# Seven products for the gated blocks of the last stage, with sums of sign matrices kept on chip

## The chip, the cores and the metric

The kernel runs on one core of one Trainium2 chip. The metric is the device time of one execution in microseconds (us). TensorE (PE) multiplies, VectorE (DVE), ScalarE (ACT) and GpSimd (POOL) do elementwise work, SyncE (SP) issues most DMAs. All data are float32.

## The reference

For x of 4 x 512 tokens and 1024 features, with 16 heads of 64:

```python
xn = layernorm(x)
s = attention(xn @ Wq, xn @ Wk, xn @ Wv) @ Wo        # rotary on q and k, causal
routing = softmax(xn @ gate_w.T)                     # 8 experts
in_scale, out_scale = routing @ in_channel_scale, routing @ out_channel_scale
g = silu(((xn * in_scale) @ sign(weight).T) * out_scale + bias)
out = x + s * g
```

The change is in the gated product `(xn * in_scale) @ sign(weight).T`, and in how its results and those of `@ Wo` are put together.

## The kernel before

**Stages.** For each of the four sequences the kernel normalizes and transposes x (and spills it as `xn_d`), projects queries, keys and values, and computes scores, probabilities and values, which it spills as `at_d`. Projections and attention are interleaved on TensorE: `interleave` deals the matmuls of the projections evenly between the "pieces" of the attention of the group before (scores, transposes, values). The projections and the product with Wo are already done by Strassen's scheme in the form with seven products: quarters of the left operand give sums S1 to S4, quarters of the right one T1 to T4, and the products 1 to 7 are combined through partial sums u2 = product 1 + product 6 and u3 = u2 + product 7.

**The last stage** works on eight pairs of row tiles (128 tokens each; a pair is `pairs[q] = (b, t)`, its tiles `t` and `t + 2` of sequence `b`). Pairs 0 and 1 have their gated product computed among the last pieces of attention. From then on, pair after pair:

- `project_out(q)`: seven products of the attention output with Wo. Each is four float32 matmuls of 512 columns, and each such matmul shows as two passes in the trace. `finish` adds the partial sums, multiplies by the gate Z and adds the residual x (`XR`), and a DMA writes the rows out.
- Between those products, `in_scales(q + 1)` scales the inputs of the next pair (`XP`) by the routing, `split` writes each as a high and a low float32r part (`hi` by ScalarE, `lo` by VectorE as input minus high part), and `out_scales` puts the output scales into Z.
- `gated(q + 1)`: for each of the four blocks (row tile i, column half k) `ffn` sums 8 chunks x 2 parts = 16 float32r matmuls of 512 columns with the stored signs `sg[0..7]` in one PSUM bank. VectorE then multiplies the bank by Z, POOL adds the bias, ScalarE takes the sigmoid, POOL multiplies.

**What sets the order.** TensorE's order is that of the program text (`manual_schedule`). The other engines are ordered by a scheduler, except for instructions under `keep_in_program_order`. Each engine works in order, so an instruction that waits holds up all behind it; SP's DMA queue is such a line too. Buffers come from pools with a fixed number of places: four PSUM banks for `bank` (the ring), four for Wo's products (`ps_wo`), one place for XP, two for the attention output (`ap0` and `app`, pairs taking turns), two each for `hi`, `lo`, `xr`, `c` and `g`.

Of the kernel before, what the change touches and what calls it, by code (L numbers as in the profile page):

```python
# [9 lines left out]
F32 = mybir.dt.float32  # L10
F32R = mybir.dt.float32r
AF = mybir.ActivationFunctionType
ALU = mybir.AluOpType
# [38 lines left out]
def attn_gated_ffn_kernel(  # L52
# [705 lines left out]
    def split(q, i):  # L758

        HI[q, i] = hl.tile([P, NC, P], F32R, tag="hi", name=f"hi_{q}_{i}")  # L760
        LO[q, i] = hl.tile([P, NC, P], F32R, tag="lo", name=f"lo_{q}_{i}")
        for c in range(0, NC, 4):
            xs, hi, lo = (v[:, c : c + 4, :] for v in (XP[q][:, i], HI[q, i], LO[q, i]))
            nc.scalar.copy(hi, xs)
            nc.vector.tensor_tensor(lo, xs, hi.bitcast(F32), op=ALU.subtract)


    z_place = {}
# [108 lines left out]
    for k, (b, g) in enumerate(groups):  # L877
        pieces = []
        if k > 0:
            pieces, late = attention_pieces(k - 1, late)  # L880
        extra = []
        if g == 0:
            routing = [lambda n=n: router(b, n) for n in range(3)]
            if k == 0:
                nothing = lambda: None
                pieces = [
                    routing[0],
                    lambda: (load_scales(in_scale), load_scales(out_scale)),
                    routing[1],
                    nothing,  # L890
                    routing[2],
                    lambda: split_scales(isc),
                    nothing,
                    nothing,
                    nothing,
                ]
            else:

                if b < B - 1:
                    pieces.insert(7, routing[0])  # L900
                pieces.insert(10, routing[1])
                pieces.insert(13, routing[2])
        elif g == 1 and b + 1 < B:

            pieces.insert(12, lambda: [load_x(b + 1, t) for t in range(2)])
            if b == 0:
                pieces.insert(6, lambda: split_scales(osc))
        elif g > 1 and b + 1 < B:
            t0 = 2 * (g - 2)
            for t in range(t0, t0 + 2):  # L910
                layernorm(b + 1, t)
            extra = [
                lambda t=t, h=h: transpose_x(b + 1, t, h) for t in range(t0, t0 + 2) for h in range(2)
            ]
            if g == 2:
                extra.append(lambda: [load_x(b + 1, t) for t in (2, 3)])

        step = max(1, (len(pieces) + len(extra)) // (len(extra) + 1))
        for n, e in enumerate(extra):
            pieces.insert(min(len(pieces), (n + 1) * step + n), e)  # L920
        if len(pieces) > 18:

            pieces.append(lambda: None)
        if k in (5, 9, 12, 13):
            n = {5: 0, 9: 2, 12: 4, 13: 6}[k]
            pieces.insert(8, lambda: make_sign(n + 1))
            pieces.insert(4, lambda: make_sign(n))
            pieces.insert(0, lambda: (load_sign(n), load_sign(n + 1)))
        if b == B - 1:

            if g < 2:
                load_xn(g)
            if g in (1, 2):
                pieces.insert(3, lambda: in_scales(g - 1, score_banks))
            if g == 3:
                z_place[0] = [xip.tile([P, E], F32, tag="x", name=f"z0_{i}") for i in range(2)]
                pieces.insert(3, lambda: out_scales(0, score_banks))
        if k == 11:

            pieces.append(lambda: router(b + 1, 0))  # L940
        interleave(pieces, fill, 3 * 7 * 4 if k else 3 * 7 * 4 - 8)
        if g == NGRP - 1:
            for _ in fill:
                pass
            if b + 1 < B:
                for n in (3, 1, 2, 4):
                    form_x(b + 1, n)
                fill = projections(b + 1)
# [45 lines left out]
    def ffn(q, i, k):  # L994

        cols = slice(k * HALF, (k + 1) * HALF)
        acc = bank(f"ff_{q}_{i}_{k}")
        for c in range(NC):
            for part in (HI, LO):
                nc.tensor.matmul(  # L1000
                    acc,
                    lhsT=part[q, i][:, c, :],
                    rhs=sg[4 * k + c // 2][:, (c % 2) * HALF : (c % 2 + 1) * HALF],
                    start=(c == 0 and part is HI),
                    stop=(c == NC - 1 and part is LO),
                )
            if c % 2 and c < NC - 1:
                yield
        z = Z[q, i][:, cols]
        nc.vector.tensor_tensor(z, acc, z, op=ALU.mult)  # L1010
        nc.gpsimd.tensor_tensor(z, z, bias_sb[:, cols], op=ALU.add)
        if q > 1:
            silu(q, i, k)
        yield

    def silu(q, i, k):
        z = Z[q, i][:, k * HALF : (k + 1) * HALF]
# [8 lines left out]

    def load_at(q):
        b, t = pairs[q]
        place = app if q % 2 else ap0
        AP_[q] = place.tile([P, 2, NC, P], F32, tag="ap", name=f"ap_{q}")  # L1030
        for i in range(2):
            nc.sync.dma_start(out=AP_[q][:, i].rearrange("p c q -> p (c q)"), in_=at_d[b, t + 2 * i])
# [57 lines left out]
    xsp = pool(side="right", name="xs", bufs=1)  # L1090
    work = pool(side="right", name="work", bufs=2)
    sp = pool(side="right", name="strassen", bufs=1)
    ps_wo = pool(side="right", name="ps_wo", bufs=4, space=PSUM)

    def form_a(q, n):
# [6 lines left out]
            3: lambda: (a11, a21, ALU.subtract),  # L1102
            4: lambda: (a12, SA[q, 2], ALU.subtract),
        }[n]()
        nc.vector.tensor_tensor(s, x0, x1, op=op)

    def project_out(q):

        b, t = pairs[q]
        rows = [slice((b * TPB + t + 2 * i) * P, (b * TPB + t + 2 * i + 1) * P) for i in range(2)]  # L1110
        for i in range(2):
            XR[i] = work.tile([P, E], F32, tag="xr", name=f"xr_{q}_{i}")
            nc.sync.dma_start(out=XR[i], in_=x[rows[i], :])
        a11, a12, a21, a22 = (AP_[q][:, i, 4 * f : 4 * f + 4, :] for i in range(2) for f in range(2))

        def product(n, lhs, rhs):
            ps = ps_wo.tile([P, HALF], F32, tag="wo", name=f"wo_{q}_{n}")
            for k in range(4):
                nc.tensor.matmul(ps, lhsT=lhs[:, k, :], rhs=rhs[:, k, :], start=(k == 0), stop=(k == 3))  # L1119
            return ps  # L1120

        def part(n):
            return sp.tile([P, HALF], F32, tag=f"part{n}", name=f"part_{q}_{n}")

        def finish(i, k, ps, u):
            cols = slice(k * HALF, (k + 1) * HALF)
            c = work.tile([P, HALF], F32, tag="c", name=f"c_{q}_{i}_{k}")
            z = Z[q, i][:, cols]
            nc.vector.tensor_tensor(c, ps, u, op=ALU.add)
            nc.vector.tensor_tensor(z, c, z, op=ALU.mult)  # L1130
            nc.gpsimd.tensor_tensor(z, z, XR[i][:, cols], op=ALU.add)

        def ahead_of(i, k, u):

            cols = slice(k * HALF, (k + 1) * HALF)
            c = work.tile([P, HALF], F32, tag="g", name=f"uz_{i}_{k}")
            nc.gpsimd.tensor_tensor(c, u, Z[q, i][:, cols], op=ALU.mult)
            nc.gpsimd.tensor_tensor(c, c, XR[i][:, cols], op=ALU.add)
            return c

        def finish_last(i, cols, ps, c, queue):
# [3 lines left out]
            queue.dma_start(out=out[rows[i], cols], in_=z)  # L1145

        yield
        ps = product(1, a11, b11)
        p1 = part(1)
        nc.scalar.copy(p1, ps)  # L1150
        ps = product(2, a12, b21)
        finish(0, 0, ps, p1)
        yield
        ps = product(6, SA[q, 2], t2)
        u2 = part(2)
        nc.vector.tensor_tensor(u2, ps, p1, op=ALU.add)
        ps = product(7, SA[q, 3], t3)
        u3 = part(3)
        nc.vector.tensor_tensor(u3, ps, u2, op=ALU.add)
        yield  # L1160
        last = q == len(pairs) - 1
        if last:
            nc.sync.dma_start(out=out[rows[0], :HALF], in_=Z[q, 0][:, :HALF])
            c10 = ahead_of(1, 0, u3)
        ps = product(5, SA[q, 1], t1)
        p5 = part(5)
        nc.scalar.copy(p5, ps)
        finish(1, 1, ps, u3)
        nc.gpsimd.tensor_tensor(u2, u2, p5, op=ALU.add)
        yield  # L1170
        ps = product(4, a22, t4)
        if not last:
            finish(1, 0, ps, u3)
            nc.gpsimd.dma_start(out=out[rows[1], :], in_=Z[q, 1])
            ps = product(3, SA[q, 4], b22)
            finish(0, 1, ps, u2)
            nc.gpsimd.dma_start(out=out[rows[0], :], in_=Z[q, 0])
            return
        c01 = ahead_of(0, 1, u2)
# [22 lines left out]
            for k in range(2):  # L1202
                silu(q, i, k)
    for q in range(len(pairs)):
        for n in range(1, 5):
            form_a(q, n)
        if q + 1 < len(pairs):
            load_at(q + 1)
        ahead = []
        if 1 <= q < len(pairs) - 1:  # L1210
            ahead = [
                lambda: None,
                lambda: (in_scales(q + 1), split(q + 1, 0), split(q + 1, 1)),
                lambda: out_scales(q + 1),
            ]
        for _ in project_out(q):
            if ahead:
                ahead.pop(0)()
        if 1 <= q < len(pairs) - 1:
            if q + 2 < len(pairs):  # L1220
                load_xn(q + 2)
            for _ in gated(q + 1):
                pass


def _rotary_tables():
# [55 lines left out]
```

## Time and profile before

| | |
|---|---|
| median of 3 runs | 1176.7 us (1176.45 to 1176.75) |
| the profiled execution | 1177.4 us, span 1175.7 us |
| busy: TensorE, weight loads | 1166.3 us (99%), 859.9 us (73%) |
| busy: VectorE, ScalarE, POOL | 754.8 us (64%), 488.0 us (42%), 555.2 us (47%) |
| granted TensorE clock | 1.0 |
| last stage, from the first product with Wo | 883.85 us to the end |
| one pair there | 39.8 us: gated 14.5, products with Wo 24.4, scales 0.9 |

Busy time is summed by engine over the span. TensorE's instructions overlap, so a busy TensorE is not one at its peak; what an instruction of it costs is read from how far a stage advances per instruction. Idle time of an engine that is not the bottleneck costs nothing by itself.

### The profile page before, as it was taken

The page shows a single profiled execution, that of the slowest core. Times are in us where ns is not written, and L with a number is a line of the kernel's source. Part 1 is how long each engine was busy: PE and PEld are TensorE (multiplying, and loading weights), DVE is VectorE, ACT ScalarE, POOL GpSimd, SP SyncE. Part 2 cuts the span into 40 slices and gives each one's busy share as a digit, 9 for nine tenths or more (in the row PEclk, how much of TensorE's full clock was granted, in tenths as well). Part 3 has the DMA queues.
Part 4 walks back from the last instruction along what each step waited for, and adds up shares of the span by engine and source line. Part 5 has one row for each costly group of instructions (what it writes and reads, how often), then busy time and mean ns, then how long its engine had stood idle before and what let it go on. Part 6 is the DMA issues. An engine that isn't in the chain of part 4 may idle for free.

```text
span 1175.7 us, 16090 instructions
## 1 busy us (share of the span) xinstructions
PE 1166.3 (99%) x5864; PEld 859.9 (73%) x5864; DVE 754.8 (64%) x1380; ACT 488.0 (42%) x1115; POOL 555.2 (47%) x597
## 2 busy tenths in 40 slices
PE   9999999999999999999999999999999999999998
PEld 8878787877878787877878787787774556655664
DVE  7876677568768667776877776665856543453343
ACT  2552673363366435436653453564532221222120
POOL 0661654264255435524643552374446445543544
PEclk9999999999999999999999999999999999999999
DMA  8413423222242232224227212211404513432320
GB/s 309 134 37 105 146 94 94 91 84 81 81 162 81 67 132 83 81 81 145 60 84 243 83 63 81 81 50 55 179 15 165 191 56 108 148 114 70 108 72 36
DMA packets 60015, 121.92 MB, mean 104 GB/s; under 512 B 5024, under 2 KB 40608, under 8 KB 53920
## 3 DMA queue, kind: packets, MB, share of 16 engines
q1 hardware_dynamic: 55072, 112.11, 28.8%
q0 software_dynamic: 4576, 8.39, 2.1%
q8 instruction: 46, 0.75, 0.2%
q10 hardware_dynamic: 288, 0.39, 0.1%
q14 instruction: 33, 0.27, 0.1%
HBM read 95.45 MB, written 25.43 MB: 103 GB/s over the span
## 4 chain that ended last, share of the span: by engine, by line
PE 96%; DVE 2%; ACT 1%; issue 1%; POOL 0%; DVEq 0%; POOLq 0%; ACTq 0%
PE pj L342 31%; PE wo L1119 16%; PE pj L429 16%; PE ff L1000 10%; PE sc L517 6%; PE pv L599 6%; PE ptp L583 6%; PE xtp L210 1%; PE idle L791 1%; PE lg L622 1%; ACT p L535 0%; DVE S L296 0%; PE os L774 0%; PE is L746 0%; DVE w L296 0%
## 5 line engine op out<-in xcount | busy, mean ns | idle before, releaser
L545 POOL TENSOR_SCALAR p<-p,rs 128x128 f32<-128x128 f32 (+3 forms) x256 | 170.3, 678 | 263.5 <-DVE rs L543 263.4
L535 ACT ACTIVATE p<-sc,nmx 128x128 f32<-128x128 f32 (+3 forms) x256 | 132.7, 524 | 155.1 <-DVE nmx L532 145.2
L342 PE MATMUL pj<-X,w 128*128 128x256 f32 x576 | 138.3, 381 | 0.2 <-ACT X L216 0.2
L326 POOL TENSOR_TENSOR sw<-sw,sin_sb 128x512 f32<-128x512 f32 x64 | 87.6, 1369 | 94.8 <-ACT sw L324 81.6
L342 PE MATMUL pj<-T,S 128*128 128x256 f32 x512 | 123.7, 382 | 0.0
L342 PEld LDWEIGHTS pj<-X,w 128*128 128x128 f32 x576 | 105.1, 190 | 14.4 <-issue 1.8
L342 PE MATMUL pj<-T,w 128*128 128x256 f32 x448 | 107.3, 381 | 0.0
L589 ACT COPY pT<-ptp 128x512 f32<-128x512 f32 x96 | 56.1, 586 | 119.4 <-PE ptp L583 118.9
L532 DVE TENSOR_REDUCE nmx<-sc 128x2 f32<-128x512 f32 (+3 forms) x128 | 103.7, 820 | 2.8
L1000 PE MATMUL ff<-sg,hi 128*128 128x512 f32 x256 | 103.3, 404 | 0.0
L342 PEld LDWEIGHTS pj<-T,S 128*128 128x128 f32 x512 | 93.2, 190 | 13.6 <-issue 1.4
L1000 PE MATMUL ff<-sg,lo 128*128 128x512 f32 x256 | 99.8, 390 | 0.0
L429 PE MATMUL pj<-w,X 128*128 128x256 f32 x416 | 97.9, 381 | 0.0
L583 PE MATMUL ptp<-ident,p 128*128 128x128 f32 x640 | 94.8, 273 | 1.2 <-ACT pT L589 1.2
L327 POOL TENSOR_TENSOR rot<-rot,sw 128x512 f32<-128x512 f32 x64 | 93.7, 1464 | 4.7
L323 ACT ACTIVATE sw<-c 32x512 f32<-32x512 f32 x128 | 80.4, 628 | 34.3 <-DVE c L356 32.2
L583 PEld LDWEIGHTS ptp<-ident,p 128*128 128x128 f32 x640 | 79.0, 141 | 17.4 <-ACT pT L589 1.4
L342 PEld LDWEIGHTS pj<-T,w 128*128 128x128 f32 x448 | 82.2, 190 | 10.7 <-issue 1.0
L429 PEld LDWEIGHTS pj<-w,X 128*128 128x128 f32 x416 | 76.6, 190 | 10.5 <-issue 1.2
L517 PE MATMUL sc<-rot,rot 64*128 64x384 f32 (+3 forms) x512 | 82.3, 450 | 1.7 <-ACT p L535 1.7
L429 PE MATMUL pj<-w,T 128*128 128x256 f32 x352 | 81.9, 383 | 0.0
L324 ACT ACTIVATE sw<-c 32x512 f32<-32x512 f32 x128 | 80.4, 628 | 1.7
(143 smaller groups left out, 1946.8 us busy)
## 6 DMA issues: line engine op xcount, KB each, us to landing
w<-in_wqk SPq DMA_DIRECT2D x31, 1024.0 KB, 5.2
w<-in_wv SPq DMA_DIRECT2D x16, 1024.0 KB, 4.8
x<-in_x SPq DMA_DIRECT2D x16, 512.0 KB, 3.7
xn_d<-X SPq DMA_DIRECT2D x16, 512.0 KB, 5.7
at_d<-v SPq DMA_DIRECT2D x32, 256.0 KB, 2.3
xp<-xn_d SPq DMA_DIRECT2D x16, 512.0 KB, 4.9
ap<-at_d SPq DMA_DIRECT2D x16, 512.0 KB, 4.3
xr<-in_x SPq DMA_DIRECT2D x16, 512.0 KB, 4.3
```

Source lines behind the costliest of these rows:

```text
L323: nc.scalar.activation(sw[r : r + 32, :], c[r + 32 : r + 64, :], AF.Copy, scale=sc)
L326: nc.gpsimd.tensor_tensor(sw, sw, sin_sb, op=ALU.mult)
L327: nc.gpsimd.tensor_tensor(rot, rot, sw, op=ALU.add)
L342: nc.tensor.matmul(ps, lhsT=wq[:, k, :], rhs=xq[:, k, :], start=(k == 0), stop=(k == 3))
L429: nc.tensor.matmul(ps[:, j, :], lhsT=xq[:, k, j * P : (j + 1) * P], rhs=wq[:, k, :], start=(k == 0), stop=(k == 3),)
L517: nc.tensor.matmul(ps[:, h, :], lhsT=Q[u][r : r + D, i * P : (i + 1) * P], rhs=K[u][r : r + D, : (i + 1) * P], start=True, stop=True,)
L532: nc.vector.tensor_reduce(nmx, ps, AX.X, ALU.max, negate=True)
L535: nc.scalar.activation(pt[:, h, :], ps[:, h, :], AF.Exp, bias=nmx[:, h : h + 1], accum_out=ssum[:, h : h + 1],)
L545: nc.gpsimd.tensor_scalar(pt[:, h, :], pt[:, h, :], rs[:, h : h + 1], 1.0, op0=ALU.mult, op1=ALU.mult,)
L583: nc.tensor.transpose(tp[:, k, :], probs(u, i)[:, h, j * P : (j + 1) * P], ident)
L1000: nc.tensor.matmul(acc, lhsT=part[q, i][:, c, :], rhs=sg[4 * k + c // 2][:, (c % 2) * HALF : (c % 2 + 1) * HALF], start=(c == 0 and part i ...
L1119: nc.tensor.matmul(ps, lhsT=lhs[:, k, :], rhs=rhs[:, k, :], start=(k == 0), stop=(k == 3))
```

## The change

- **Gated blocks of pairs 2 to 7** are computed with seven products instead of eight quarter products. The left quarters are a11, a12 (row tile 0, feature halves), a21, a22 (row tile 1), with S1 = a21 + a22, S2 = S1 - a11, S3 = a11 - a21, S4 = a12 - S2, the same form as for Wo (S2 is stored over a11 and S4 formed over a12). The operands a11 and S2, a12 and S3, S1 and a22, and S4 are split into high and low parts, two operands to a tile.
- **Sums of signs** T1 to T4 are formed once by VectorE (`sign_sum`), T1 to T3 during pair 0 and T4 after pair 1. T3 overwrites `sg[4]` and `sg[5]`; T1 and T2 get a pool of their own; T4 takes the place `app`, so from pair 2 on the attention output has one place (`ap0`) and is loaded later.
- **Two products in one bank**: product 2 is summed onto product 1, and product 3 onto product 5, after those have been read, in the gated blocks and for Wo. The order for Wo is 1, 6, 2, 7, 5, 4, 3.
- **The residual** is loaded in quarters (128 x 512) instead of two row tiles.
- The forms `form_a` of pairs from 2 on move into the gated block and are pinned, as are the low parts of pair 0 (`sub`). In the second group of attention an empty piece is inserted, which moves later pieces back.

```diff
-            nc.vector.tensor_tensor(lo, xs, hi.bitcast(F32), op=ALU.subtract)
+            sub = nc.vector.tensor_tensor(lo, xs, hi.bitcast(F32), op=ALU.subtract)
+            if q == 0:
+                tc.keep_in_program_order(sub)
...
                 pieces.insert(6, lambda: split_scales(osc))
+                pieces.insert(1, lambda: None)
...
-        place = app if q % 2 else ap0
+        place = app if q == 1 else ap0
...
+    def sign_sum(n):
+        if n == 3:
+            TS[n] = [sg[4], sg[5]]
+        else:
+            t = (app if n == 4 else tsp).tile(
+                [P, 2, E], F32R, tag="ap" if n == 4 else f"T{n}", name=f"Tsg{n}"
+            )
+            TS[n] = [t[:, r, :] for r in range(2)]
+        for r in range(2):
+            x0, x1 = {
+                1: lambda: (sg[4 + r], sg[r]),
+                2: lambda: (sg[6 + r], TS[1][r]),
+                3: lambda: (sg[6 + r], sg[4 + r]),
+                4: lambda: (sg[2 + r], TS[2][r]),
+            }[n]()
+            nc.vector.tensor_tensor(
+                TS[n][r], x0.bitcast(F32), x1.bitcast(F32), op=ALU.subtract
+            )
...
+    def parts(q, *operands):
+        tiles = [
+            hl.tile([P, NC, P], F32R, tag=tag, name=f"{tag}_{q}_{operands[0][0]}") for tag in ("hi", "lo")
+        ]
+        for j, (name, xs) in enumerate(operands):
+            if name == "S2":
+                s1, a11 = xs
+                nc.vector.tensor_tensor(a11, s1, a11, op=ALU.subtract)
+                xs = a11
+            hi, lo = PARTS[q, name] = [v[:, 4 * j : 4 * j + 4, :] for v in tiles]
+            nc.scalar.copy(hi, xs)
+            nc.vector.tensor_tensor(lo, xs, hi.bitcast(F32), op=ALU.subtract)
...
+        parts(q, ("a11", a11), ("S2", (a21, a11)))
+        return lambda: parts(q, ("a12", a12), ("S3", s3))
...
+        one = product("a11", signs11, 1)
+        p1 = part(1)
+        nc.scalar.copy(p1, one)
+        ps = product("S2", TS[2], 6)
+        u2 = part(2)
+        nc.vector.tensor_tensor(u2, ps, p1, op=ALU.add)
+        parts(q, ("S1", a21), ("a22", a22))
+        gate(q, 0, 0, product("a12", signs21, 2, one))
+        ps = product("S3", TS[3], 7)
+        u3 = part(3)
+        nc.vector.tensor_tensor(u3, ps, u2, op=ALU.add)
+        nc.vector.tensor_tensor(a12, a12, a11, op=ALU.subtract)
+        parts(q, ("S4", a12))
+        five = product("S1", TS[1], 5)
+        summed(1, 1, five, u3)
+        for n in range(1, 5):
+            form_a(q, n)
+        summed(1, 0, product("a22", TS[4], 4), u3)
+        summed(0, 1, product("S4", signs22, 3, five), u2)
...
-        ps = product(1, a11, b11)
+        one = product(1, a11, b11)
         p1 = part(1)
-        nc.scalar.copy(p1, ps)
-        ps = product(2, a12, b21)
-        finish(0, 0, ps, p1)
-        yield
+        nc.scalar.copy(p1, one)
         ps = product(6, SA[q, 2], t2)
         u2 = part(2)
         nc.vector.tensor_tensor(u2, ps, p1, op=ALU.add)
+        yield
+        finish(0, 0, product(2, a12, b21, one))
...
-            ps = product(3, SA[q, 4], b22)
-            finish(0, 1, ps, u2)
+            finish(0, 1, product(3, SA[q, 4], b22, five), u2)
```

In `gated_by_strassen`, `product` runs four chunks with a high and a low part each; `summed` adds the partial sum into `c` and calls `gate`, which holds the four steps (VectorE times Z, POOL bias, sigmoid, POOL product). `first_parts` (S3, S1 and the four first operands) is called where `split` was, in two halves.

## The prediction

> **What bounds the kernel now.** I read the busy table first, then TensorE's waits, then the chain of waits through the last stage, then the timeline of one pair.
>
> ```profile
> PE 1166.3 (99%) x5864; PEld 859.9 (73%) x5864; DVE 754.8 (64%) x1380; ACT 488.0 (42%) x1115; POOL 555.2 (47%) x597
> ```
>
> TensorE's waits (total, times, longest):
>
> ```profile
> PE sc L517 <- ACT p L535: 1.7, 1, 1.7
> PE ptp L583 <- ACT pT L589: 1.2, 1, 1.2
> ```
>
> The chain that ended last (start, us, what):
>
> ```profile
> 987.79 6.87 PE wo L1119 x16
> 994.65 0.44 PE is L746 x6
> 995.09 7.07 PE wo L1119 x16
> 1002.15 0.44 PE os L774 x4
> 1002.59 10.50 PE wo L1119 x24
> 1013.09 14.54 PE ff L1000 x64
> 1027.63 6.87 PE wo L1119 x16
> ```
>
> TensorE is busy 99% and waits in only two places after the start: 1.7 us at a score product (61.3 to 63.0) and 1.2 us at a transpose (830.2 to 831.4). In the last stage the chain is TensorE alone: one pair takes 1027.63 - 987.79 = 39.84 us, 14.54 of it for 64 gated matmuls (0.2272 us each) and 24.4 for 28 output products of two passes each (0.432 us a pass). So matmuls taken from the gated block come off the end, as long as nothing new makes TensorE wait.
>
> **The change, part by part.** Durations are of the profiled execution: span 1175.7, its own time 1177.4, which is 0.7 over the median of the three runs, 1176.7. The sum is made against 1177.4.
>
> *Gated block.* Seven products of 4 chunks x 2 parts are 56 matmuls for 64, in six pairs (2 to 7): 48 fewer. The built order agrees, 1893 TensorE rows for 1941. By the row above: 48 x 0.2272 = 10.9 us. The Trainium skill ("TensorE: Matmul & The Clock Gate", Back-to-back issue gap) gives some 131 ns for a sustained 512-column matmul with its weight load, and 216 ns for one without; 48 of these would be 6.3 or 10.4 us. The row is this shape in this stage, so I take 10.9; 10.4 goes into the range.
>
> *The piece put into the second group.* It sets the later pair of score products eight matmuls (16 passes of 0.216 us, 3.5 us) further on. The stalled one wanted to start at 61.3 and was released by the exponential of the first scores at 63.0. It now comes at 64.8 and the bank is free: -1.7. What is late next: the two 128x1024 weight forms now stand ahead of the scores' mask on VectorE, about 2.5 us, but the transposes of these scores only come at 98. Bounds: 0 and -1.7.
>
> *Pinned low parts of pair 0.* In the trace a low part (828.65, 0.95 us) stands ahead of the row maximum at 829.52, for which ScalarE idled 0.37 us before the copies that release the transpose. It now comes after: -0.4 of the 1.2. Bounds: 0 and -0.8.
>
> *Does VectorE keep up?* It has 17.3 us of work in 40 per pair (26 instructions). Per pair the change adds four sums (S1 to S4), three low parts, two u sums and three c sums, and takes one c sum away: 11 more, at 0.61 us a step back to back some 7 us: 24 to 27 of 38. ScalarE gets 3 high parts and a copy more and one copy less, POOL one sum less. No engine becomes the bound on average; order decides, so I walk it. The steps come from these lines:
>
> ```profile
> 1016.79 0.69 DVE L1010 TENSOR_TENSOR z<-ff,z 128x512 f32<-128x512 f32 x1 [1.70 <-PE ff L1000]
> 1017.57 1.28 POOL L1011 TENSOR_TENSOR z<-z,bias_sb 128x512 f32<-128x512 f32 x1 [0.22 <-DVE z L1010]
> 1018.89 0.63 ACT L1019 ACTIVATE g<-z 128x512 f32<-128x512 f32 x1 [12.04 <-POOL z L1011]
> 1019.60 1.29 POOL L1020 TENSOR_TENSOR z<-z,g 128x512 f32<-128x512 f32 x1 [0.74 <-ACT g L1019]
> ...
> 1002.80 0.68 DVE L1105 TENSOR_TENSOR S<-ap 128x512 f32<-128x512 f32 x1
> 1006.93 1.26 POOL L1169 TENSOR_TENSOR part<-part,part 128x512 f32<-128x512 f32 x1 [1.76 <-ACT part L1167]
> 1007.49 1.25 DVE L1105 TENSOR_TENSOR S<-S,ap 128x512 f32<-128x512 f32 x1
> ```
>
> Gate, bias, sigmoid and product follow each other at 0.69, 1.28, 0.63, 1.29 with gaps of 0.2 to 0.3, 0.04 and 0.08. And a VectorE sum of two SBUF operands takes 0.68 alone but 1.25 beside a POOL sum: it ends 0.55 after POOL does.
>
> *The new chain in the gated block.* Let TensorE begin product 1 at 0. Each product is 1.82: 6 ends at 3.64, 2 at 5.46, 7 at 7.27, 5 at 9.09, 4 at 10.91, then 3. Product 3 needs the high and low parts of S4, and, since it is summed into the bank of 5, the end of the VectorE sum that reads 5. ScalarE's order puts the sigmoid of block (0,0) ahead of the high part of S4. VectorE: u2 at 3.84 (0.2 after the product), low S1 4.45, low a22 5.1, gate (0,0) 5.71 to 6.40. POOL bias 6.70 to 7.98; sigmoid 8.02 to 8.65; high S4 to 9.20 (0.55); POOL's product 8.72 to 10.0. Low S4 starts at 9.25 beside it: 1.25 by the row, 10.5. The sum c(1,1) reads a PSUM bank and one SBUF operand (0.69 in every row, beside POOL too): 11.1; with a semaphore 11.16. TensorE wants it at 10.91: **0.25 us of stall per pair, 1.5 in six.** Below: 0. Above: "SBUF - State Buffer" (Who interferes with whom) says that the two engines' shared read port is an exclusive lock for a whole instruction, which speaks against putting more two-operand sums on VectorE: a low part that met the start of POOL's product would take 1.29 + 0.68 = 1.97, not 1.25, a stall of 0.97 per pair and 5.8 in all. The row applies, as POOL's start and low S4 follow the same sigmoid 0.07 and 0.6 later; 5.8 is the upper end.
>
> *What else waits behind it.* Forms for the next output products stand behind c(1,1): z(1,1) 11.7, S1 12.7, c(1,0) 13.3, S2 14.0 (up to 15 beside POOL). Output product 6 needs S2 at 13.0 + 3.46 = 16.4. z(1,0) is at 16.5, bias 18.1, sigmoid 18.7, the copy of output product 1 behind it on ScalarE 19.3; product 2, summed into that bank, wants it at 20.3. Free. The first four low parts are done some 30 us after product 1, when TensorE still has 7 us of output products. S1 and a22 reuse the first tile as soon as 6 is read: low S1 at 5.1, wanted at 7.27. Free.
>
> *DMA and queues.* One attention tile in place of two: the next load waits for output product 4 (21.6 us into the output products), lands 4.3 later and is wanted by a form at about 37: 11 us spare. The inputs of the next pair are loaded after S4 is split (10.5 into the gated block), land 4.9 later at 15.4 and are wanted at 20. The residual comes in four quarters, two of them only issued when POOL has freed one; on SP they stand behind the inputs and ahead of the attention load. The last quarter is issued 3.6 before the block ends, and lands at +0.7 by the 4.3 of a load twice its size; POOL wants it at 1.9. Cost nothing, with some 1 us of cover, and 4.1 before it delays the bias above.
>
> *Sums of signs.* Six VectorE sums of 128x1024 in pair 0, two in pair 1. The nearest rows (weight forms of that size) take 1.22 alone. From 890.2 to 901 POOL multiplies eight sigmoids without a gap, so five of the six take twice that, as the forms of half that size do there (1.38 and 1.45 for 0.68): 2.45. From 889.0: 890.2, 892.7, 895.1, u2 895.8, 898.2, 900.7, z(0,0) 901.3. TensorE wants z's bank for product 4 at 901.1: 0.3. The sixth, u3 and a form follow, c(1,1) ends at 905.2, wanted at 904.9: 0.4. **+0.7**, between 0 (no overlap) and 3.5 (half a us more each). The two in pair 1 end at 26.2 and leave c(0,1) 2 us of cover before u2: 0.
>
> *Output products, tail.* Their number stays; summing two in one bank drops a VectorE sum, a copy and a POOL sum that cover hid: 0. In the last pair u2 still gets p5 from POOL; the last quarter lands about 22 after its product 1, the term built from it is ready at 23.6, needed by 24.8: 0.
>
> **Sum:** -10.9 - 1.7 - 0.4 + 1.5 + 0.7 = -10.8. 1177.4 - 10.8 = 1166.6, against the median 0.7 less: **1166.0**.
>
> **The rivals.**
> 1. *The S4 chain eats the gain* (0.22): a stall of about 0.97 per pair instead of 0.25. For it: five hand-overs between four engines with no slack. Against: the row for the sum beside POOL. 4.3 more: 1170.3.
> 2. *Sums of signs stall the first two pairs* (0.08): at 3.5 for 0.7, 1168.8; up to 1171 if bank and order delay each other. Against: VectorE idles for 8.7 us there today (889 to 908).
> 3. *Slower, by POOL's queue* (0.05): POOL works in order; if the last residual quarter lands late, its add, the output issue behind it (0.6), the bias of (0,0), the sigmoid and S4's high part all wait, and TensorE with them. Harmless to +4.8 (6.70 less 1.28 and 0.6); each us beyond costs 1 us in each pair. It cancels 10.8 us from 1.8 per pair on, landing at +6.6: 10.2 us after its issue. At 12 us after issue it is 3.6 a pair, 10.8 lost net: 1187. Against: residual loads took 4.3, of 512 KB, and the DMA share is 0.24 to 0.54 here.
> 4. *Nothing comes of it* (0.03): 1 and 2 at their worst and no gain at the start. That the matmuls are not saved is excluded by the built order.
>
> **How the numbers follow.** The likeliest case has 0.62. Its best: -10.9 - 1.7 - 0.8 with no new stall is -13.4, 1163.3; its worst, 10.4 saved, nothing at the start and both stalls doubled, about 1170.7. To take in rival 1 and most of 2 the range reaches 1171.5. Outside lie rivals 3, 4 and some of 2 and of the best ends. About 0.2% (2.4 us) is what a measurement of this kernel can tell from no change. Faster 0.92, same 0.03, slower 0.05.
>
> **What would show it.** Right: six gated blocks of 12.7 to 13.0 us on the chain and a pair of about 38.3; the wait at the scores gone; a wait of TensorE on VectorE of some 0.2 to 0.3 us before each product 3, none before output products 2 and 6. Low S4 near 1.25 us and not 0.68. Wrong if TensorE waits over 0.6 in each block, if POOL waits for a residual DMA, if the sums of signs show over 2.6 us each, or if a matmul of the gated block takes over 0.23.

## The result, and the profile after

The changed kernel takes 1170.2 us (median of 6 runs, 1169.2 to 1170.4), the kernel before 1176.6 (6 runs, 1175.8 to 1177.6): a ratio of 0.9942, 95% interval 0.9932 to 0.9952. The prediction was 1166.0, inside a range of 1163.3 to 1171.5: the sign and the main mechanism held, and 4.2 us of the gain are missing. The profiled execution spans 1168.6 us (1175.7 before) and took 1170.4 itself.

The page of the changed kernel, busy time of each engine (us, share of the span, instructions):

```profile
PE 1159.0 (99%) x5816; PEld 851.2 (73%) x5816; DVE 826.0 (71%) x1452; ACT 496.8 (43%) x1132; POOL 559.8 (48%) x590
```

TensorE still bounds everything. One pair of the last stage, from the chain that ended last (start, us, what):

```profile
986.41 6.87 PE wo L1243 x16
...
993.72 7.06 PE wo L1243 x16
...
1001.22 10.50 PE wo L1243 x24
1011.72 13.10 PE ff L1183 x56
1024.81 6.87 PE wo L1243 x16
```

A pair takes 1024.81 - 986.41 = 38.40 us for 39.84, and all of the 1.44 is in the gated block: 56 matmuls in 13.10 us where 64 took 14.54. Six pairs give 8.6 us. The two earlier pairs take 49.53 us in both kernels (883.85 to 933.38 before, 885.37 to 934.90 after), and from the last gated block's end to the end of the span it is 28.5 and 28.6. So 8.6 us are gained in the last stage, and the whole is only 7.1 faster by the spans: something in front of it became slower. The waits of TensorE (engine, line, waited for: us in total, times, longest) name it:

```profile
PE pj L429 <- DVE w L296: 2.6, 1, 2.6
...
PE ptp L583 <- ACT pT L589: 0.3, 1, 0.3
```

The wait at the scores (1.7) has gone as forecast, the one at the transpose fell from 1.2 to 0.3, and a new one of 2.6 us stands at 92 us: TensorE waits for VectorE to form a sum of value weights. That place is in the second group of projections, 800 us ahead of the Strassen products.

VectorE's own order around it in the changed kernel (start, us, engine, line, operation; an idle time before it in brackets):

```profile
86.61 0.17 DVE L543 RECIPROCAL rs<-ssum 128x2 f32<-128x2 f32 x1 [0.88 <-ACT p L535]
86.70 0.69 DVE L296 TENSOR_TENSOR S<-w 128x512 f32<-128x512 f32 x1
87.30 0.69 DVE L691 CAST osc<-scales 128x1024 fp32r<-128x1024 f32 x1
87.90 0.78 DVE L296 TENSOR_TENSOR w<-w 128x512 f32<-128x512 f32 x1
88.61 0.86 DVE L692 TENSOR_SCALAR scales<-scales,row_kind 128x1024 f32<-128x1024 f32 x1
89.39 0.67 DVE L296 TENSOR_TENSOR S<-w 128x512 f32<-128x512 f32 x1
89.99 1.27 DVE L694 SCALAR_TENSOR_TENSOR osc<-osc,row_kind,scales 128x1024 fp32r<-128x1024 f32 x1
...
92.51 0.67 DVE L296 TENSOR_TENSOR S<-w,S 128x512 f32<-128x512 f32 x1
93.11 1.74 DVE L296 TENSOR_TENSOR w<-w 128x1024 f32<-128x1024 f32 x1
```

A form is one of Strassen's sums of quarters, here of weights; L296 makes them. The last line is S4 of the value weights. Ahead of it, from 86.70 on, VectorE works without a gap: half-size forms (128x512) of the weights that come next, the output scales and sums of v. What starts this row is the reciprocal at 86.61, the end of the delayed scores' softmax. Before, the same row started at 84.22, and its last line waited for TensorE instead of the other way round. VectorE and then TensorE of the kernel before:

```profile
91.13 1.22 DVE L296 TENSOR_TENSOR w<-w 128x1024 f32<-128x1024 f32 x1 [0.53 <-PE pj L429]
```

```profile
94.38 3.62 PE L429 MATMUL pj<-w,X 128*128 128x256 f32 x16
```

So the form ended at 92.35 and was wanted at 94.38: it had two us of slack, the time by which it could have been later at no cost. In the changed kernel TensorE is there 2.1 us sooner, at 92.26 (1.7 of it the stall at the scores, the rest an earlier start of this run), and the form comes 2.5 us later, at 94.85. TensorE, and then the stretches (length; busy time and instructions of PE, PEld, DVE, ACT, POOL; granted clock; DMA share; GB/s), of the changed kernel:

```profile
94.90 5.41 PE L429 MATMUL pj<-w,X 128*128 128x256 f32 x16 [2.64 <-DVE w L296]
```

```profile
92.00:94.00 2.00, 0.26 (x2) 0.00 (x0) 2.00 (x4) 1.87 (x2) 1.30 (x2) 1.00 0.84 250
94.00:96.00 2.00, 1.10 (x4) 1.01 (x5) 2.00 (x5) 0.00 (x0) 1.43 (x1) 0.91 0.36 57
96.00:98.00 2.00, 2.00 (x6) 1.56 (x6) 1.58 (x4) 0.29 (x1) 0.00 (x0) 0.50 0.71 279
98.00:100.00 2.00, 2.00 (x9) 1.64 (x8) 0.00 (x0) 0.00 (x0) 0.00 (x0) 0.74 0.48 201
```

The wait is paid twice. After it the granted clock falls to 0.50 (0.91 and 0.74 are stretches that have it in part), and the 16 matmuls that took 3.45 us up to the next transpose (94.38 to 97.83) take 5.24 (94.90 to 100.14): 1.79 us more. 2.64 + 1.79 - 1.67 saved at the scores is a loss of 2.8 us where a gain of 1.7 was forecast. This is the theory to test. Its rival: the late form comes from another part of the change (the pinned low parts, say), and the piece is worth its 1.7 us.

### The profile page after: what moved, and what is told of

Read it like the earlier page. It is cut to its first block, busy times and chain, and to the rows that moved or that the text cites. A ratio compares the mean times of both kernels' runs of the same rounds, so it can differ in the third digit from the quotient of the medians.

```text
span 1168.6 us, 16127 instructions
## 1 busy us (share of the span) xinstructions
PE 1159.0 (99%) x5816; PEld 851.2 (73%) x5816; DVE 826.0 (71%) x1452; ACT 496.8 (43%) x1132; POOL 559.8 (48%) x590
## 3 DMA queue, kind: packets, MB, share of 16 engines
q1 hardware_dynamic: 57376, 112.11, 28.6%
## 4 chain that ended last, share of the span: by engine, by line
PE 92%; DVE 3%; ACT 2%; issue 1%; POOL 1%; POOLq 0%; DVEq 0%; ACTq 0%
PE pj L342 31%; PE wo L1243 15%; PE pj L429 15%; PE ff L1183 7%; PE pv L599 6%; PE sc L517 6%; PE ptp L583 6%; PE ff L1004 3%; PE xtp L210 1%; ACT p L535 1%; PE idle L793 1%; DVE S L296 1%; PE lg L622 1%; DVE w L296 1%; ACT sw L324 1%
## 5 line engine op out<-in xcount | busy, mean ns | idle before, releaser
L599 PE MATMUL pv<-pT,v 128*64 128x256 f32 (+3 forms) x512 | 76.0, 439 | 0.0
L528 DVE TENSOR_TENSOR sc<-sc,mask 128x256 f32<-128x256 f32 x128 | 53.8, 420 | 28.7 <-PE sc L517 28.4
```

The lines of the kernel that those rows point to most:

```text
L599: nc.tensor.matmul(pv[r : r + D, j * P :], lhsT=V[u][:, j, r : r + D], rhs=PT[u][:, n, o : o + (TPB - j) * P], start=(j == 0), stop=(j == ...
```

## The experiments

All times are medians, with the runs of the kernel before beside them on the same chip.

| kernel | us | before | ratio, 95% interval |
|---|---|---|---|
| changed | 1170.2 | 1176.6 | 0.9942 (0.9932 to 0.9952) |
| changed, without the piece | 1168.0 | 1176.8 | 0.9921 (0.9908 to 0.9933) |
| before, with the piece alone | 1179.1 | 1176.8 | 1.0020 (1.0013 to 1.0026) |
| before, with the pin alone | 1175.8 | 1176.8 | 0.9990 (0.9984 to 0.9997) |
| changed, output scales early | 1166.5 | 1176.8 | 0.9913 (0.9900 to 0.9927) |
| changed, S4 form pinned | 1166.0 | 1176.3 | 0.9911 (0.9896 to 0.9925) |
| changed, both remedies | 1165.1 | 1176.3 | 0.9903 (0.9888 to 0.9918) |
| both, and S4's high part first | 1164.4 | 1176.3 | 0.9898 (0.9882 to 0.9915) |
| the last, tiles of the last stage moved 32 bytes | 1164.2 | 1176.5 | 0.9894 (0.9877 to 0.9910) |
| S4 first, all right-hand tiles moved 32 bytes | 1164.2 | 1176.5 | 0.9892 (0.9877 to 0.9907) |
| S4 first, sums of signs in other places | 1164.5 | 1176.8 | 0.9897 (0.9880 to 0.9913) |
| before, left-hand tiles moved 32 bytes | 1176.5 | 1176.5 | 0.9999 (0.9990 to 1.0008) |

Where the intervals of two kernels overlap, as among the remedies below, their medians do not tell them apart, and what is said of the difference rests on the traces.

### Without the piece

```diff
-                pieces.insert(1, lambda: None)
```

> The changed kernel without the empty piece in the second group. Theory: the piece took away a 1.7 us wait of TensorE at the scores, but its delay of the scores pushed VectorE's S4 form of the value weights late, which cost a 2.6 us wait and, since the granted clock fell to 0.50 after it, about 1.9 us more of slow products. Without the piece the 1.7 us wait is back and 4.5 us go: about 1167.3 us, granted clock 1.0 through 92 to 100 us, no wait of TensorE on the value weights. Rival (the piece is worth its 1.7 us, and the late form has another cause in the change, such as the pinned low parts): about 1171.9 us, the 2.6 us wait still there.

1168.0 us, 2.2 less than the changed kernel; the two intervals just touch. Its longest wait of TensorE:

```profile
PE sc L517 <- ACT p L535: 1.7, 1, 1.7
```

and no wait on the value weights; the granted clock is 1.00 in every stretch from 90 to 100 us. The theory's figure was 1167.3, the rival's 1171.9. Taking the forecast gain away made the kernel faster by the medians; the next run shows the same on the kernel before, clear of noise.

### The piece alone, on the kernel before

```diff
             if b == 0:
                 pieces.insert(6, lambda: split_scales(osc))
+                pieces.insert(1, lambda: None)
```

> The kernel before with the empty piece alone. Theory: slower by 4.5 less 1.7, 2.3 to 2.9 us, about 1179.2 us, with the 2.6 us wait on the value weights and a granted clock near 0.5 behind it. Rival (as the prediction had it, the piece is a gain and the late form comes from another part of the change): 1.7 us faster, about 1174.9 us, no new wait.

1179.1 us, 2.3 slower, and the interval leaves out no change. TensorE, and the stretches behind the wait:

```profile
94.07 5.25 PE L429 MATMUL pj<-w,X 128*128 128x256 f32 x16 [2.70 <-DVE w L296]
```

```profile
94.00:96.00 2.00, 1.93 (x5) 1.57 (x6) 2.00 (x7) 0.00 (x0) 0.60 (x1) 0.50 0.39 78
96.00:98.00 2.00, 2.00 (x8) 1.65 (x7) 0.74 (x2) 0.29 (x1) 0.00 (x0) 0.70 0.96 406
```

The same wait and the same fall of the clock, with no Strassen and no pin in the program. The rival is out: the piece does it by itself.

### The pin alone, on the kernel before

```diff
-            nc.vector.tensor_tensor(lo, xs, hi.bitcast(F32), op=ALU.subtract)
+            sub = nc.vector.tensor_tensor(lo, xs, hi.bitcast(F32), op=ALU.subtract)
+            if q == 0:
+                tc.keep_in_program_order(sub)
```

> The kernel before with only the low parts of the first pair pinned to program order. Theory: the wait of TensorE at the transpose falls from 1.2 us to about 0.3: 0.8 to 0.9 us faster, about 1175.7 us. As the prediction had it: 0.4 us. Rival (the 0.8 us between 98 and 884 us in the two traces have nothing to do with the pin): no difference, the wait of 1.2 us still there.

1175.8 us, 1.0 faster, and the wait at the transpose is 0.3 us where it was 1.2. By the trace the pin is worth twice the 0.4 of the forecast, about its bound of 0.8; the interval (0.4 to 1.9 us) shows a gain and leaves its size open.

### The output scales early

```diff
                     routing[2],
                     lambda: split_scales(isc),
-                    nothing,
+                    lambda: split_scales(osc),
...
-                pieces.insert(6, lambda: split_scales(osc))
+                pieces.insert(6, lambda: None)
```

> The changed kernel with VectorE's work on the output scales (three operations, about 2.8 us) moved from the second group to the first, an empty piece left in its place so that TensorE's order is the same. Theory: the S4 form of the value weights is late because the delayed scores and this block of 2.8 us both stand ahead of it on VectorE; without the block it is done before TensorE wants it. Both waits, at the scores and at the value weights, are gone and the clock stays at 1.0: about 1165.5 us. Rival (the scores alone make the form late, or the block delays something in the first group instead): the form still late by 1 us or more, or a new wait in the first group, 1168 to 1171 us.

1166.5 us, 3.7 less than the changed kernel, and 1.0 over the theory's figure. TensorE and its clock:

```profile
92.69 3.72 PE L429 MATMUL pj<-w,X 128*128 128x256 f32 x16 [1.32 <-DVE w L296]
```

```profile
92.00:94.00 2.00, 1.31 (x6) 1.18 (x7) 2.00 (x6) 0.84 (x1) 1.92 (x2) 1.00 0.25 41
94.00:96.00 2.00, 2.00 (x11) 1.77 (x10) 1.37 (x3) 0.30 (x1) 0.00 (x0) 1.00 0.84 324
```

Neither theory had it whole. 2.8 us less work ahead of the form shortened the wait by only 1.3. From 60 us on VectorE's line has the same steps at the same distances here as in the changed kernel, but it lies 1.4 us later against TensorE: the first row maximum of the delayed scores starts 5.27 us after those scores (72.76 to 78.03) and not 3.87 (73.66 to 77.53). So half of what was moved came back as a later line out of the first group, which was part of the rival. But with 1.3 us of wait the clock stays at 1.00, and the second half of the cost is gone entirely.

### The form pinned ahead of work that nobody waits for

```diff
-        nc.vector.tensor_tensor(f, x0, x1, op=op)
+        form = nc.vector.tensor_tensor(f, x0, x1, op=op)
+        if (*key, n) in ((0, 0, 2, 4), (0, 2, 0, 1), (0, 2, 0, 2)):
+            tc.keep_in_program_order(form)
```

> The changed kernel with three weight forms of the second group pinned in VectorE's order: the S4 form of the value weights ahead of two half-size forms of the next key (S1, S2) that the scheduler had put before it, and S4 of the values itself; nothing else is moved. The forms of the next key are wanted much later. Theory: the late form is a matter of what stands ahead of it in VectorE's line; three forms of 0.7 to 0.8 us, about 2.1 us, less ahead of it leave a wait of 0.1 to 0.6 us of the 2.6, too short for the clock to fall: 4 us faster than the changed kernel, about 1166.3 us. Rival (the line is late because of the scores' chain, which the forms only fill while it waits): the form starts no earlier, 1170 us.

1166.0 us for 1166.3. VectorE and TensorE:

```profile
91.45 1.22 DVE L296 TENSOR_TENSOR w<-w 128x1024 f32<-128x1024 f32 x1
```

```profile
92.72 3.72 PE L431 MATMUL pj<-w,X 128*128 128x256 f32 x16 [0.41 <-DVE w L296]
```

The scores and the scales are where they were; three half-size forms behind the S4 form instead of ahead of it leave 0.4 us of the 2.6. The form was late by its place in VectorE's line, and the rival (it starts no earlier) is out. In the expectations, a "key" is the program's name for one set of weights.

> Both remedies together: the output scales' work on VectorE moved to the first group, and the S4 form of the value weights pinned ahead of the two half-size forms of the next key. The kernel with the scales moved alone took 1166.5 us with 1.3 us of wait at this form. Theory: three half-size forms less ahead of it, about 2.1 us, and the form is done before TensorE wants it: no wait, 1.2 to 1.3 us faster than with the scales moved alone, about 1165.2 us. Rival (the form must then wait for TensorE's own reading of the buffer that it overwrites): 0.5 us or more of the wait stays, 1165.9 or over.

With both remedies the wait is gone (the 16 matmuls start at 91.59 with no idle time before them) and the kernel takes 1165.1 us. The median is 1.4 below that of the scales alone, with overlapping intervals; the spans are 1164.6 and 1163.2. As no wait is left, that rival (the form waits for TensorE's own reading) is out.

### The high part of S4 ahead of the sigmoid

This asks for the term that the forecast put at 0.25 us per pair. The changed kernel's steps between products 7 and 3, all engines but TensorE:

```profile
1018.12 1.29 POOL L1020 TENSOR_TENSOR z<-z,bias_sb 128x512 f32<-128x512 f32 x1 [2.61 <-DVE z L1019]
...
1019.44 0.63 ACT L1027 ACTIVATE g<-z 128x512 f32<-128x512 f32 x1 [3.07 <-POOL z L1020]
...
1019.98 0.60 ACT L1156 CAST hi_S<-xp 128x512 fp32r<-128x512 f32 x1
...
1020.15 1.30 POOL L1028 TENSOR_TENSOR z<-z,g 128x512 f32<-128x512 f32 x1 [0.74 <-ACT g L1027]
...
1020.62 1.38 DVE L1157 TENSOR_TENSOR lo_S<-xp,hi_S 128x512 fp32r<-128x512 f32 x1 [0.82 <-ACT hi_S L1156]
...
1021.92 0.68 DVE L1198 TENSOR_TENSOR cf<-ff,part_ff 128x512 f32<-128x512 f32 x1
```

The walk of the forecast is all there, in its order: the high part waits behind the sigmoid, the low part meets POOL's product and ends 0.55 us after it, the sum that frees product 5's bank comes last and ends at 1022.60, about when product 4 does. The experiment puts the high part first:

```diff
-        gate(q, 0, 0, product("a12", signs21, 2, one))
+        gate(q, 0, 0, product("a12", signs21, 2, one), silu_now=False)
...
         parts(q, ("S4", a12))
+        silu(q, 0, 0)
```

with ScalarE's high part of S4 and this sigmoid kept in program order.

> As the kernel with both remedies, and in each gated block ScalarE takes the high part of S4 ahead of the sigmoid of block (0,0). Theory: the stall of TensorE before product 3, about 0.1 us in each of six pairs, goes: the high part can start at the end of product 7, some 1 us earlier, and the low part no longer meets POOL's product, 0.68 us for 1.38. 0.5 to 0.8 us faster than both remedies without it, about 1164.6 us, and the start of product 3 follows product 4 at 1.87 us and not 1.95 to 1.98. Rival (the 0.1 us belongs to the bank of product 5 or to the hand-over and not to S4): no difference, 1.95 stays.

1164.4 us for 1164.6. The same steps in it, and then one gated block on the chain, of the kernel with both remedies and of this one:

```profile
1013.05 0.62 ACT L1159 CAST hi_S<-xp 128x512 fp32r<-128x512 f32 x1 [2.51 <-PE ff L1188]
...
1013.59 0.64 ACT L1028 ACTIVATE g<-z 128x512 f32<-128x512 f32 x1
1013.89 0.68 DVE L1162 TENSOR_TENSOR lo_S<-xp,hi_S 128x512 fp32r<-128x512 f32 x1
1014.30 1.42 POOL L1031 TENSOR_TENSOR z<-z,g 128x512 f32<-128x512 f32 x1 [0.74 <-ACT g L1028]
...
1015.14 0.69 DVE L1203 TENSOR_TENSOR cf<-ff,part_ff 128x512 f32<-128x512 f32 x1 [0.57 <-PE ff L1188]
```

```profile
1044.72 13.09 PE ff L1184 x56
```

```profile
1044.12 12.94 PE ff L1188 x56
```

The low part runs clear of POOL at 0.68, the sum now waits for product 5 and not for S4, and the blocks take 12.92 to 12.94 for 13.09 to 13.10. So the S4 stall was 0.16 us per pair, 1.0 in six, which is the difference of the two spans (1163.2 and 1162.2). Product 3 starts 1.86 to 1.87 us after product 4 where it was 1.95 to 1.97, so the rival is out.

### Why some products take 1.87 us

12.94 is still not 7 x 1.817 = 12.72, seven products at the rate of the kernel before (14.54 / 64 for a matmul). In the changed kernel, the first matmul of each product from 6 on (6, 2, 7, 5, 4), where `Tsg` is a tile of a sum of signs of its own and `sg` one of the signs (T3 lies in the place of one, so product 7 reads `sg`):

```profile
1013.40 0.40 PE L1183 MATMUL ff<-Tsg,hi_a 128*128 128x512 f32 x1
...
1015.27 0.40 PE L1183 MATMUL ff<-sg,hi_a 128*128 128x512 f32 x1
...
1017.09 0.39 PE L1183 MATMUL ff<-sg,hi_a 128*128 128x512 f32 x1
...
1018.90 0.40 PE L1183 MATMUL ff<-Tsg,hi_S 128*128 128x512 f32 x1
...
1020.77 0.40 PE L1183 MATMUL ff<-Tsg,hi_S 128*128 128x512 f32 x1
```

Products 6 and 5 take 1.87 us, 2 and 7 take 1.82. First question: is it what they read, or their buffers and place in the sequence? The moving operand, in the texts below, is the right-hand side that a matmul streams, here the signs or their sums.

```diff
-        gate(q, 0, 0, product("a12", signs21, 2, one))
+        gate(q, 0, 0, product("a12", TS[2], 2, one))
...
-        ps = product("S2", TS[2], 6)
+        ps = product("S2", signs21, 6)
```

> The changed kernel with the right-hand sides of products 2 and 6 of the gated block exchanged: product 6 reads the signs of the second quarter, product 2 the sum of signs T2 (so another function is computed). Only the spacing of the matmuls is asked. In the changed kernel products 6, 5 and 4 (right-hand side in the tiles of T2, T1, T4) take 1.87 us for 8 matmuls, products 2 and 7 (signs, and T3, which lies in a tile of signs) 1.82. Theory A, the tile that is read: product 6 takes 1.82 and product 2 takes 1.87. Theory B, the buffer of the high and low parts (6, 5 and 4 use the first, 2 and 7 the second) or the place in the sequence: as before, 1.87 and 1.82. No change of the time is expected from either (below 0.1 us).

Product 6 took 1.81 to 1.82 and product 2 1.86 to 1.87, in all six pairs: theory A, the tile that is read. (One run, 1169.3 us.) The tiles with 1.87 begin 32 bytes over a multiple of 64 in memory, those with 1.82 at a multiple. Three runs asked whether that is it. The pad, ahead of the last stage's pools, ahead of the signs of the kernel before, and ahead of all right-hand pools:

```diff
+    pad = pool(side="right", name="pad", bufs=1).tile([P, 8], F32, name="pad")
+    nc.vector.memset(pad, 0.0)
     app = pool(side="right", name="ap", bufs=1)
```

> As the kernel with both remedies and the high part of S4 first, with an unused tile of 32 bytes per partition put ahead of the last stage's right-hand pools, which moves all their tiles by 32 bytes. In the program the tiles of T1, T2 and T4 begin at addresses that are 32 over a multiple of 64 bytes, those of the signs (and T3) at multiples of 64; with the pad all are multiples of 64. Theory (the address of the moving operand sets the 1.87 us): products 6, 5 and 4 take 1.82, 0.15 us less per gated block, 0.9 us in six: 1163.5 us against 1164.4. Rival (it is the memory region or the shape of the tile, not the 32 bytes): 1.87 stays, no difference.

> The kernel before with an unused tile of 32 bytes per partition ahead of the signs, which moves the signs, the transposed input, the weights and their sums, Wo's parts and its sums from multiples of 64 bytes to 32 over such a multiple. Theory: each matmul of the gated block takes 0.2333 us for 0.2272, 14.9 us a block for 14.54, 2.3 us in six and 0.8 in the first two; whether the float32 passes (two for each product) pay too is open: 0 if not, and if a pass of 512 columns pays the same 0.006 us, some 2 us more in the output products and up to 15 in the projections. So 1180 us or more. Rival (not the address): no difference, 1176.5.

> As the kernel before this one but one in the list (remedies, S4 first, pad in the last stage), with the same pad of 32 bytes put once ahead of all right-hand pools, so that the rotated queries and keys, the values and the probabilities of the attention stage are moved to multiples of 64 bytes too. Scores and products with the values are busy for 182 us in the changed kernel. If their passes pay as the gated block's do (2.7%), up to 4.9 us less than with the pad in the last stage alone: 1158.6 to 1163.5. If the float32 passes do not pay, the same time within 0.3 us.

(The "kernel before this one but one" is that of the first of these three.) All three say no. With the pad in the last stage products 6 and 5 still take 1.87 and a block 12.93; with everything on the right moved the time is the same, 1164.2; and the kernel before with its left-hand tiles moved off the multiple takes 1176.5 against 1176.5, its gated blocks 14.53 to 14.56. The address modulo 64 is not the cause. The last run changes places instead:

```diff
-        if n == 3:
+        if n == 2:
             TS[n] = [sg[4], sg[5]]
         else:
-            t = (app if n == 4 else tsp).tile(
+            t = (ap0 if n == 4 else tsp).tile(
...
-        place = app if q == 1 else ap0
+        place = ap0 if q == 0 else app
```

> The kernel with both remedies and S4 first, with the sums of signs in other places: T2 takes the tile of signs that T3 had, T3 takes the tile that T2 had, and T4 lies in the attention output's first place instead of its second (the attention loads of pairs 2 to 7 take the second). In the changed kernel the products of T1, T2 and T4 take 1.87 us for eight matmuls, that of T3 1.82. Place theory (the region of memory that the moving operand is in): product 6 (T2) 1.82, product 7 (T3) 1.87, product 5 (T1) 1.87 as before; product 4 (T4), whose new place lies between those of the two kinds, is open, 1.82 or 1.87. Content theory (what the sums hold): 6, 5 and 4 stay at 1.87, 7 at 1.82. The time: 1164.4 us with content, up to 0.3 us less with place.

First matmuls of products 6, 2, 7, 5, 4, 3:

```profile
1008.23 0.39 PE L1188 MATMUL ff<-sg,hi_a 128*128 128x512 f32 x1
...
1010.05 0.39 PE L1188 MATMUL ff<-sg,hi_a 128*128 128x512 f32 x1
...
1011.86 0.40 PE L1188 MATMUL ff<-Tsg,hi_a 128*128 128x512 f32 x1
...
1013.73 0.40 PE L1188 MATMUL ff<-Tsg,hi_S 128*128 128x512 f32 x1
...
1015.60 0.39 PE L1188 MATMUL ff<-Tsg,hi_S 128*128 128x512 f32 x1
...
1017.43 0.39 PE L1188 MATMUL ff<-sg,hi_S 128*128 128x512 f32 x1
```

T2, now among the signs, takes 1.82; T3, now on the right, takes 1.87; T1, which stayed on the right, 1.87; T4, in a place between, 1.83, where it took 1.87 before (product 4 of the kernel with S4 first). The place in memory sets the rate and not what the sums hold; nor the form of the tile, as T4's is the same in both places. In the program the signs lie 29 to 62 thousand bytes up in each partition, T4's new place at 158 to 167, T1 and T3 at 168 to 184, T4's old place above those (no trace shows an address). The block is 12.87 and the time the same within the measurement, 1164.5.

The 1.83 is no third rate. In other pairs a product from the signs takes that much too, where it follows one of 1.87: product 2, behind product 6, in the fourth gated block of the changed kernel, its first matmul and that of product 7:

```profile
1053.67 0.39 PE L1183 MATMUL ff<-sg,hi_a 128*128 128x512 f32 x1
...
1055.51 0.39 PE L1183 MATMUL ff<-sg,hi_a 128*128 128x512 f32 x1
```

That is 1.84. T4's product follows product 5 with its 1.87, so its new place cannot be told from that of the signs.

## Why the prediction was right, and where it was wrong

Its sum was -10.8 against a measured -7.1 (spans; -6.4 in the medians). Two small slips in it change nothing: 1176.7 - 10.8 is 1165.9 and not 1166.0, and a pass of the output products is 24.4 / 56 = 0.436 us and not 0.432.

- **Gated block, -10.9 and +1.5: -9.4 forecast, -8.6 measured.** The 48 matmuls went, at the row's price: products from the signs still take 1.82 for eight, 0.2275 each. Neither the 131 nor the 216 ns of the Trainium skill ("TensorE: Matmul & The Clock Gate", Back-to-back issue gap) appears in this shape; the page gives the 216 for an isolated matmul. The S4 stall was 0.16 a pair for 0.25, for the reason given, and the low part beside POOL took 1.38 for 1.25: the 1.97 of rival 1 did not come; POOL's product had run 0.47 us of its 1.30 when the low part started, which accounts for most of the difference. What the sum lacked: three products read at 0.233 us a matmul because of where their sums of signs lie, 3 x 0.05 x 6 = 0.9 us. The sum of these terms is 12.72 + 0.16 + 0.15 = 13.03. Products 2 and 3, from the signs but behind products of 1.87, take up to 0.02 more each; the last 0.03 of the 13.10 I can't assign. The block is just outside the 12.7 to 13.0 that the prediction named as the sign of being right.
- **The piece put into the second group, -1.7: this is the step that failed.** It was +2.8 in the trace, +2.2 and +2.3 us by taking it away and by adding it alone. The stall did go, as worked out. "What is late next" was the error. The prediction looked for the next one who needs the delayed scores, found the transposes at 98 us, and called it free. It did not ask who stands behind the delayed scores in VectorE's line. There stood S4 of the value weights, with 2 us of slack; the delay took 2.5, and TensorE arrived 2.1 sooner. And "bounds: 0 and -1.7" left out a loss with no reason that excluded one. Delaying a piece of work can cost more than it saves.
- **The pin, -0.4: -0.9 in the trace, -1.0 in the medians.** The right wait and the right cause, half the size. With the pin the row maximum starts 0.03 us after the first of these transposes, for 0.81 before (829.52 and 828.71), and ScalarE's copies start 0.5 sooner against it; TensorE gets one group of four transposes further before it must wait for a copy, and then waits 0.3. The forecast counted only ScalarE's idle 0.37.
- **Sums of signs, +0.7: 0.** Pairs 0 and 1 take 49.53 us in both kernels. Rival 2 is out. The forecast gave five of the six sums 2.45 us each; most took 1.2 to 1.7, one 2.28.
- **Output products, tail, residual loads, 0: 0.** The output part of a pair is 25.30 in both (39.84 - 14.54 and 38.40 - 13.10). No POOL sum waited for a residual load (one issue of an output by POOL, at 914.0 us, shows 0.3 us put down to one), so rival 3 is out too.

Leaving the failed step aside, the other terms come to -9.5 (-8.6 - 0.9) against -9.1 forecast: their errors cancel. With the 2.8 of the failed step, and TensorE's rows 0.3 us earlier from the start in this run, they give -7.0.

That 1170.2 lies inside the range is partly luck. The range reached 1171.5 to make room for the S4 chain and the sums of signs; those cost 1.0 and nothing, and a loss that the prediction did not foresee took their room. One of the signs that the prediction named for being wrong did show, a matmul of the gated block over 0.23 us, in the three products that read from the right. The version with both remedies and S4's high part first takes 1164.4 us, 5.8 below the changed kernel, and the intervals of the two ratios (0.9882 to 0.9915 and 0.9932 to 0.9952) do not meet. Three of the runs after it differ from it by less than their intervals.

## What to carry to other kernels

When you move work later to give its input time, follow two lines from it: who needs its result, and who stands behind it on each engine that it uses, down to the first instruction with less slack than the delay; a stall that you remove upstream takes its length off that slack too. Add the clock to the price of a wait: here 2.6 us of idle TensorE cost 4.4. If something has to be late, pin the instruction that TensorE wants next ahead of those wanted later; that took three lines and gave back at least as much as leaving the piece out (1166.0 and 1168.0 us, with overlapping intervals): the stall at the scores stayed away, and 0.4 us of the new wait was left.

## What the runs showed of the hardware

The granted clock: with waits of TensorE of 2.64, 2.65 and 2.70 us it fell to 0.50, with 1.67 and 1.32 us it did not. Read in stretches of half a us, the fall lasted 3.4 us each time; it began 0.7 and 0.1 us after the end of the first two waits and 0.3 us before the end of the third. Its cost follows: 3.4 us at half the clock lose 1.7 us of work, near the 1.79 measured in the changed kernel. The Trainium skill ("TensorE: Matmul & The Clock Gate", What's actually happening) has the gate fall to half after at least one idle window of about 3.4 us. The half is what the traces show; that a wait shorter than the window is enough is this case's number, and what happens between 1.7 and 2.6 us no run here shows.

The rate of a one-pass matmul of 512 columns depended on where its moving operand lies: eight took 1.81 to 1.84 us from the place of the signs and from T4's place at 158 thousand bytes, and 1.86 to 1.87 from 168 to 184 and from T4's place above, whatever the contents, the form of the tile and the address modulo 64. That is 2.7% (1.87 for 1.82). Why is open, and so is where between the two places the rate changes; for the float32 products no run here tells it.
